# Two-layer graph attention on one core: moving five of sixteen destination blocks of the edge counting to ScalarE's steps, and re-dealing the first stage's order

## The chip, the core and the metric

The kernel runs on one core of a Trainium2 chip. The engines are TensorE (PE, with its weight loads shown as PEld), VectorE (DVE), ScalarE (ACT), GpSimd (POOL) and SyncE (SP); each takes its instructions in the order in which they were recorded and waits on semaphores where an instruction needs another engine's result. The metric is the device time of one execution in microseconds (us); the time given is the median over runs. All times below, unless said otherwise, are from the start of the span of the one profiled execution.

## What is computed

512 nodes with 768 features, 16896 edges sorted by destination (512 of them self loops). Layer 1 has 8 heads of 768 columns, layer 2 has one:

```
def gat_layer(x, W, a_s, a_d, b, edge_index, concat):
    h = (x @ W).reshape(n, H, C)
    alpha_s = einsum('nhc,hc->nh', h, a_s);  alpha_d = einsum('nhc,hc->nh', h, a_d)
    e = leaky_relu(alpha_s[src] + alpha_d[dst], 0.2)
    m = segment_max(e, dst);  e = exp(e - m[dst])
    alpha = e / (segment_sum(e, dst)[dst] + 1e-16)
    out = segment_sum(h[src] * alpha[:, :, None], dst)
    return out + b
h = elu(gat_layer(x, W1, a_src1, a_dst1, b1, ...));  out = gat_layer(h, W2, ...)
result = layernorm(x + out)
```

Since the edges enter only through the attention sums, the kernel turns them once into a dense 512 x 512 matrix of counts (how many edges lead from node s to node d), and from then on works with dense matrices.

## The kernel before

**Heads.** Everything is done head by head in float32. Each large product (x by W1, attention by features, features by W2) is done with seven half-size products P1 to P7 in place of eight, with sums of the operands made by VectorE or by accumulating DMAs. One such half product is three matmuls of 128x384 (`product`, L301-306), run twice (i = 0, 1, the two halves of 128 rows).

**The first stage** (up to about 62.6 us) does three things side by side: it loads and transposes x, it makes head 0's projection and the first four products of head 1's, and it counts the edges. The counting works on 132 chunks of 128 edges. For a chunk there are two one-hot matrices: 32 columns for the destination within a block of 32 nodes (`odw`, made for a quarter of the chunks at once by L493), and 512 columns for the source (`os`). A matmul of the two (L543) adds the chunk to the 32 rows of its block in a PSUM bank. Four blocks of 32 rows make a tile t of 128 destinations; the four column groups of TensorE take a matmul each, so `count` (L532-550) keeps four queues, one for each place of a block in its tile, and takes one from each in a round.

**Two kinds of source matrix.** For tiles 0, 1 and 3 VectorE makes `os` as "node equals source" (L517). For tile S = 2 ScalarE makes it as Sign(node + 0.5 - source) (L515), a step from -1 to 1; the counts of tile 2 then come out as steps, and `counted_by_steps` (L399-406) takes them out of PSUM with half weight (L403, L404, on ScalarE), subtracts neighbours (L405, on VectorE) and makes the mask `absent` (L406). For the other tiles `counted` (L394-397) copies counts and mask straight out of PSUM on ScalarE. A chunk whose edges may fall into two blocks is counted in both; where one of these is a step block and the other isn't, it needs both kinds. All `os` tiles of both kinds come from one pool of 32 buffers (L513); a buffer is free again when the last matmul that reads it is done.

**The order** is written out by hand (L566-617). The chunks are dealt into nine batches (L569: how many of the other tiles', how many of tile 2's). For each batch n the loop records: VectorE's one-hots of the batch, with the sums of products that had been waiting put into their middle (`sources`, L522-528); extra work (operand sums, and `logits`, two passes over 768 columns for each tile of nodes); the batch's projection products (`items`, up to `wants[n]`), each followed by ScalarE's copy out of PSUM and by a share of ScalarE's steps for batch n+1 (`ahead`, L599-601); and then the counting matmuls of batch n. When a tile of destinations is complete, its `counted` instructions are recorded right there (L547-550). After the last batch's products come `spread(0)` (four transposes that lay out the source logits), and then the head loop.

**Names.** In the texts c0 to c8 are the counting matmuls of batches 0 to 8; P1, P5, P3 ... without a mark are head 0's products, P1', P2', P6' head 1's. D0 to D8 are VectorE's one-hots of a batch.

**Around it.** `turn_x` (L200-206) transposes half a tile of x on TensorE into one of three PSUM buffers and copies it out on ScalarE. The P6 and P7 products of head 0 accumulate on the banks `held` that P1 used; VectorE's L428 empties the bank before the next product may start. `nidx` (L505) is the bias of ScalarE's steps. The loads of the stage go through SP's queue (L90, L144, L146, L148, L151, L158) and, for half of x, ScalarE's queue (L143); eight DMA semaphores are used in turn, so a load waits until the eighth before it has landed.

Of the kernel before, what the change touches and what calls it, by code (L numbers as in the profile page):

```python
# [13 lines left out]
AF = mybir.ActivationFunctionType  # L14
ALU = mybir.AluOpType
# [5 lines left out]
NO_EDGE = -1e30  # L21
# [15 lines left out]
def gat_pass(  # L37
# [16 lines left out]
    nc = tc.nc  # L54
# [83 lines left out]
    def block(m, r, cols):  # L138
        return m[r * HK * P:(r + 1) * HK * P, cols].rearrange("(k p) d -> p k d", p=P)

    w1_0 = w1[:, :D]
    for r, cols in enumerate((L, R)):
        nc.scalar.dma_start(x_sb[:, :2, cols], x[:2 * P, cols].rearrange("(t p) d -> p t d", p=P))  # L143
        nc.sync.dma_start(W1[0][r][:, :, L], block(w1_0, r, L))  # L144
    for t in (2, 3):
        nc.sync.dma_start(x_sb[:, t, :], x[t * P:(t + 1) * P, :])  # L146
    b1_rows = ohp.tile([H * DC, P], F32, name="b1_rows")
# [63 lines left out]
    if general:  # L211
        nc.vector.tensor_copy(idx_f, idx_i)
        idx = ohp.tile([P, 2, EC], F32, name="idx")
        psi = tr.tile([P, 512], F32, name="tr")
        for j in range(2):
            for r in range(2):
                nc.tensor.transpose(psi[:, (2 * j + r) * EH:(2 * j + r + 1) * EH], idx_f[:, j, r, :],
                                    ident[:EH, :EH])
        nc.vector.tensor_copy(idx, psi[:, :2 * EC].rearrange("p (j c) -> p j c", j=2))
    else:  # L220

        B, SLACK = 32, 10
        blocks = []
        for c in range(EC):
            m = (c + 0.5) * P * N / E
            b = int(m // B)
            lo, hi = b - (m - b * B < SLACK), b + ((b + 1) * B - m < SLACK)
            blocks.append(range(max(lo, 0), min(hi, N // B - 1) + 1))  # L230
        at = [0]
        for b in blocks:
            at.append(at[-1] + len(b))
        NB = at[EC]
        assert NB + EC <= 512 and max(map(len, blocks)) <= 2


        pick = ohp.tile([EH, NB], F32, name="pick")
        base = ohp.tile([P, NB], F32, name="base")
        lo = 0  # L240
        while lo < EC:
            hi, k = lo + 1, len(blocks[lo])
            while hi % EH and blocks[hi] == blocks[lo]:
                hi += 1
            copy = nc.vector.tensor_copy if lo < 5 * EC // 8 else nc.scalar.copy
            copy(pick[:, at[lo]:at[hi]].rearrange("p (c k) -> p c k", k=k),
                 ident[:EH, lo % EH:(hi - 1) % EH + 1].unsqueeze(2).to_broadcast([EH, hi - lo, k]))
            for j, b in enumerate(blocks[lo]):
                nc.gpsimd.memset(base[:, at[lo]:at[hi]].rearrange("p (c k) -> p c k", k=k)[:, :, j], float(b * B))
            lo = hi  # L250
        nc.vector.tensor_copy(idx_f, idx_i)
        turn_x(0, 0)
        turn_x(1, 0)
        psi = tr.tile([P, 512], F32, name="tr")
        for r in range(2):
            cols = slice(at[r * EH], at[(r + 1) * EH])
            nc.tensor.matmul(psi[:, cols], idx_f[:, 0, r, :], pick[:, cols], start=True, stop=True)
        for r in range(2):
            nc.tensor.transpose(psi[:, NB + r * EH:NB + (r + 1) * EH], idx_f[:, 1, r, :], ident[:EH, :EH])
        rel = ohp.tile([P, NB], F16, name="rel")  # L260
        nc.vector.tensor_tensor(rel, psi[:, :NB], base, op=ALU.subtract)
        idx = ohp.tile([P, EC], F32, name="idx")
        nc.vector.tensor_copy(idx, psi[:, NB:NB + EC])
# [132 lines left out]
        nc.scalar.copy(cnt[:, t, :], ps[:, :N])  # L396
        nc.scalar.activation(absent[:, t, :], ps[:, :N], AF.Relu, bias=far, scale=NO_EDGE)

    def counted_by_steps(t, ps):  # L399


        steps = ohp.tile([P, N + 1], F32, name="steps")
        nc.scalar.activation(steps[:, 1:], ps[:, :N], AF.Copy, scale=0.5)  # L403
        nc.scalar.activation(steps[:, :1], ps[:, N - 1:N], AF.Copy, scale=-0.5)  # L404
        nc.vector.tensor_tensor(cnt[:, t, :], steps[:, 1:], steps[:, :N], op=ALU.subtract)  # L405
        nc.scalar.activation(absent[:, t, :], cnt[:, t, :], AF.Relu, bias=far, scale=NO_EDGE)  # L406

    def first_projection(h, XA, B_):

# [65 lines left out]
    if not general:  # L475


        S = 2
        order = {False: [], True: []}
        for g in range(NT):  # L480
            rs = [[c for c in range(EC) if int((c + 0.5) * P * N / E) // B == b] for b in range(g * 4, g * 4 + 4)]
            while any(rs):
                order[g == S] += [r.pop(0) for r in rs if r]
        hits = {}
        for b in (b for bs in blocks for b in bs):
            hits[b] = hits.get(b, 0) + 1
# [15 lines left out]
            nc.vector.scalar_tensor_tensor(below, rel, 0.0, below, op0=ALU.is_ge, op1=ALU.mult, accum_out=found)  # L502

        nidx = ohp.tile([P, EC], F32, name="nidx")
        nc.scalar.activation(nidx, idx, AF.Copy, bias=0.5, scale=-1.0)  # L505

        def by_steps(b):
            return b * B // P == S

        hot = {}  # L510

# [20 lines left out]
        def count(batch, rest):  # L532


            for c, b in ((c, b) for c in batch for b in blocks[c]):
                queues[b * B % P // B].append((c, b, hot[c, by_steps(b)]))
            while any(queues) and (rest or all(queues) or sum(map(len, queues)) > 3):
                for c, b, h_ in [q_.pop(0) for q_ in queues if q_]:
                    t, r = b * B // P, b * B % P
                    if t not in cps:  # L540
                        pool, name = (bc, "bc") if t == S else (tr, "tr")
                        cps[t] = pool.tile([P, 512], F32, name=name)
                    nc.tensor.matmul(cps[t][r:r + B, :N], od[:, at[c] + b - blocks[c][0], :], h_,  # L543
                                     start=todo[b] == hits[b], stop=todo[b] == 1,
                                     tile_position=(0, r), skip_group_check=True)
                    todo[b] -= 1
            for t in range(NT):  # L547
                if t not in done and all(todo[b] == 0 for b in range(t * P // B, (t + 1) * P // B)):
                    (counted_by_steps if t == S else counted)(t, cps[t])
                    done.add(t)  # L550


# [13 lines left out]
        B1 = {}  # L566
        wants = [3, 4, 7, 10, 12, 14, 16, 18]
        batches = []
        for ours, theirs in ((16, 0), (8, 8), (8, 8), (12, 4), (12, 4), (12, 4), (13, 3), (14, 2), (4, 0)):  # L569
            take = [order[k][:m] for k, m in ((False, ours), (True, theirs))]  # L570
            del order[False][:ours], order[True][:theirs]
            batches.append(take[0][:ours // 2] + take[1] + take[0][ours // 2:])
        assert not any(order.values())
        pos, made, quarter, waiting = 0, set(), EC // NT, []
        for n, batch in enumerate(batches):
            for k in sorted({c // quarter for c in batch} - made):
                destinations(k * quarter, (k + 1) * quarter)
                made.add(k)
            sources(kinds(batch, False), waiting)
            ahead = kinds(batches[n + 1], True) if n + 1 < len(batches) else []  # L580
            items_here = max(wants[n] - pos if n < len(wants) else 0, 1)
            share = -(-len(ahead) // items_here)
            waiting = []
            for f in extra.pop(n, []):
                f()
            while n < len(wants) and pos < wants[n]:
                if pos == wholes:
                    pairs = projection(1, XA, B1)
                    items += [(m, e, False) for m, e in pairs[:4]]
                multiply, empty, on_vector = items[pos]  # L590
                multiply()
                if on_vector:
                    waiting.append(empty)
                else:
                    empty()
                pos += 1
                for t, r in turns.get(pos, []):
                    turn_x(t, r)
                for c in ahead[:share]:  # L599
                    one_hot(c, True)  # L600
                del ahead[:share]
            assert not ahead
            if n == 2:
                turn_b1()
            if n + 1 == len(batches):
                spread(0)
                q = [lift(0, t) for t in range(NT)]
                for t in range(NT - 1):
                    leak(q[t])
                for t in range(NT - 1):  # L610
                    rank(q[t], t)
            if n == 0:
                pst = mm.tile([P, 512], F32, name="mm")
                nc.tensor.matmul(pst[:1, :1], found, ones, start=True, stop=True)
            if n == 3:
                again = nc.values_load(flag[:1, :1], min_val=0, max_val=E)
            count(batch, n + 1 == len(batches))
# [475 lines left out]
```

## Time and profile before

| | us |
|---|---|
| median of 3 runs | 650.8 (650.75 to 650.86) |
| the profiled execution | 650.37 |
| its span, first to last instruction | 648.6 |
| TensorE busy in the span | 637.7 |
| VectorE busy | 519.6 |
| ScalarE busy | 277.3 |
| granted TensorE clock | 0.999 |

A row of the profile names a line of the kernel, an engine, an operation and the tiles it writes and reads; the bracket behind a row says how long the engine had been idle before it and what ended that. The stretches view gives each engine's busy time in a stretch of the span. The waits view adds up who waited for whom.

### The profile page before, as it was taken

How to read it: one execution, taken by the hardware profiler on the slowest of the kernel's cores; microseconds unless marked ns; L12 is line 12 of the kernel's file. 1: busy time of each engine (PE TensorE's matmuls, PEld its weight loads, DVE VectorE, ACT ScalarE, POOL GpSimd, SP SyncE). 2: the span in 40 equal slices, each digit the busy share in tenths (PEclk: the TensorE clock that was granted, in tenths of full speed). 3: DMA queues.
4: the chain of work that ended last, by engine and by line, in shares of the span. 5: the costliest groups of instructions: out<-in, count | busy, mean ns of one | idle time of the engine just before them, and what ended most of it. 6: DMA issues, size and time to landing. Idle time of an engine off the chain costs nothing.

```text
span 648.6 us, 7216 instructions
## 1 busy us (share of the span) xinstructions
PE 637.7 (98%) x2383; PEld 405.0 (62%) x2383; DVE 519.6 (80%) x1141; ACT 277.3 (43%) x482; POOL 48.3 (7%) x90
## 2 busy tenths in 40 slices
PE   8999999999999999999999999999999999999995
PEld 4544586556765586556765586556755586644553
DVE  7989989977779677877779687877779687876775
ACT  6774744530726045430726045430726045243440
POOL 1310020011000110011000110011000110000000
PEclk9999999999999999999999999999999999999999
DMA  9993499197806792196806792196706892000122
GB/s 318 328 203 86 75 327 292 35 256 207 202 0 153 170 277 97 33 260 200 205 1 149 174 277 98 33 258 204 202 1 153 218 254 97 25 1 1 29 61 76
DMA packets 77640, 97.95 MB, mean 151 GB/s; under 512 B 37094, under 2 KB 60446, under 8 KB 77598
## 3 DMA queue, kind: packets, MB, share of 16 engines
q1 hardware_dynamic: 63934, 75.80, 37.5%
q0 software_dynamic: 12976, 20.65, 18.4%
q10 hardware_dynamic: 688, 0.98, 0.4%
q8 instruction: 21, 0.34, 0.2%
q14 instruction: 21, 0.17, 0.1%
HBM read 85.09 MB, written 1.57 MB: 134 GB/s over the span
## 4 chain that ended last, share of the span: by engine, by line
PE 96%; ACT 1%; DMA 1%; DVE 1%; issue 0%; SPq 0%
PE mm L305 64%; PE mm L764 20%; PE mm L710 3%; PE mm L1039 3%; PE held L305 2%; PE tr L543 1%; DMA w<-in_L_gnn_W_dram 1%; ACT os L515 1%; PE bc L446 0%; PE bc L543 0%; PE tr L963 0%; PE tr L679 0%; ACT xT L205 0%; DVE os L517 0%; PE bc L985 0%
## 5 line engine op out<-in xcount | busy, mean ns | idle before, releaser
L305 PE MATMUL mm<-w,gT 128*128 128x384 f32 x288 | 97.5, 488 | 0.0
L305 PE MATMUL mm<-w,xT 128*128 128x384 f32 x264 | 88.2, 488 | 0.0
L305 PEld LDWEIGHTS mm<-w,gT 128*128 128x128 f32 x288 | 54.0, 190 | 35.2 <-issue 1.6
L305 PEld LDWEIGHTS mm<-w,xT 128*128 128x128 f32 x264 | 50.0, 190 | 35.4 <-ACT os L515 0.8
L768 ACT COPY u<-mm 128x256 f32<-128x256 f32 x21 | 7.8, 372 | 142.0 <-PE mm L764 142.0
L463 ACT ACTIVATE q<-q,nmax 128x512 f32<-128x512 f32 x36 | 25.8, 721 | 89.8 <-DVE nmax L461 89.8
L764 PE MATMUL mm<-PT,hs 128*128 128x256 f32 x252 | 61.4, 380 | 0.0
L305 PE MATMUL mm<-w1t,gS 128*128 128x384 f32 x180 | 60.7, 486 | 0.0
L305 PE MATMUL mm<-w2t,xS 128*128 128x384 f32 x168 | 56.6, 487 | 0.0
L764 PEld LDWEIGHTS mm<-PT,hs 128*128 128x128 f32 x252 | 47.9, 190 | 8.3 <-issue 0.4
L363 DVE TENSOR_TENSOR h<-h,mm 128x384 f32<-128x384 f32 x72 | 39.7, 551 | 14.6 <-PE mm L305 14.0
L305 PEld LDWEIGHTS mm<-w1t,gS 128*128 128x128 f32 x180 | 34.2, 190 | 23.5
L305 PEld LDWEIGHTS mm<-w2t,xS 128*128 128x128 f32 x168 | 31.9, 190 | 22.4 <-ACT q L452 0.4
L764 PE MATMUL mm<-pS,gS 128*128 128x256 f32 x168 | 43.3, 380 | 0.0
L687 ACT COPY nr<-q 128x1024 uint16<-128x1024 uint16 x32 | 33.4, 1044 | 22.9 <-DVE q L673 15.8
L692 ACT COPY PT<-zr 128x1024 uint16<-128x1024 uint16 x32 | 37.1, 1160 | 2.0 <-DMA zr<-nr 2.0
L764 PEld LDWEIGHTS mm<-pS,gS 128*128 128x128 f32 x168 | 31.9, 190 | 4.7 <-DVE pS L737 0.4
L305 PE MATMUL mm<-w,gS 128*128 128x384 f32 x96 | 32.6, 486 | 0.0
L305 PE MATMUL mm<-w1t,gT 128*128 128x384 f32 x96 | 32.5, 488 | 0.0
L305 PE MATMUL mm<-w,xS 128*128 128x384 f32 x96 | 32.5, 488 | 0.0
L106 POOL DMA_DIRECT2D w1t<-in_L_gnn_W_dram x7 | 8.9, 1267 | 311.3 <-DVE hs L727 97.8
L363 DVE TENSOR_TENSOR u<-u,mm 128x384 f32<-128x384 f32 x28 | 15.4, 553 | 19.0 <-PE mm L305 18.7
(189 smaller groups left out, 1086.1 us busy)
## 6 DMA issues: line engine op xcount, KB each, us to landing
w<-in_L_gnn_W_dram SPq DMA_DIRECT2D x90, 384.0 KB, 6.1
w<-in_L_gnn_W_dram POOLq DMA_DIRECT2D x16, 576.0 KB, 9.5
w2t<-in_L_gnn_W_dram SPq DMA_DIRECT2D x10, 576.0 KB, 4.9
w1t<-in_L_gnn_W_dram SPq DMA_DIRECT2D x9, 576.0 KB, 4.6
w2t<-in_L_gnn_W_dram POOLq DMA_DIRECT2D x8, 576.0 KB, 9.8
w1t<-in_L_gnn_W_dram POOLq DMA_DIRECT2D x7, 576.0 KB, 8.7
a_s<-in_L_gnn_a_src_dram SPq DMA_DIRECT2D x8, 384.0 KB, 3.7
a_d<-in_L_gnn_a_dst_dram SPq DMA_DIRECT2D x8, 384.0 KB, 4.1
```

Of the source, the lines that this page charges most:

```text
L106: nc.gpsimd.dma_start(t1, upper[:, :, R], accum_op=ALU.add)
L305: nc.tensor.matmul(ps[:, :HALF], A_[p][:, k, i * P:(i + 1) * P], B_[p][:, k, :], start=start and k == 0, stop=k == HK - 1, skip_group_chec ...
L363: nc.vector.tensor_tensor(a, a, ps, op=ALU.subtract if p == "P7" else ALU.add)
L463: nc.scalar.activation(q, q, AF.Exp, bias=nmax, scale=-1.0)
L515: nc.scalar.activation(o, nodes, AF.Sign, bias=nidx[:, c:c + 1])
L543: nc.tensor.matmul(cps[t][r:r + B, :N], od[:, at[c] + b - blocks[c][0], :], h_, start=todo[b] == hits[b], stop=todo[b] == 1, tile_position ...
L687: nc.scalar.copy(apart.rearrange("p (h n) -> p h n", h=2), q.bitcast(U16).rearrange("p (n h) -> p h n", h=2))
L692: nc.scalar.copy(PT.rearrange("p s n -> p (s n)").bitcast(U16).rearrange("p (s n h) -> p s n h", s=NT, h=2)[:, :, t * P:(t + 1) * P, :], p ...
L710: nc.tensor.matmul(ps[:, :N], HS[h][:, s, c * P:(c + 1) * P], PT[:, s, :], start=(s == 0), stop=(s == NT - 1))
L764: nc.tensor.matmul(bank[p][:, :HN], A_[p][:, k, c * P:(c + 1) * P], B_[p][:, k, :], start=over is None and k == 0, stop=k == 1, skip_group ...
L768: nc.scalar.copy(u, part("P1"))
L1039: nc.tensor.matmul(ps[:, :cols.stop - cols.start], PT[:, s, t * P:(t + 1) * P], h2[:, s, cols], start=(s == 2), stop=(s == 1))
```

## The change

- **First W1 part in three loads** (L144): the left half of the upper W1 block is loaded as three DMAs of 128 x 384, one for each k, in place of one of 128 x 3 x 384. Two DMAs more go through SP's queue and the eight semaphores.
- **Indices ahead of x's second transpose** (L253): `turn_x(1, 0)` is recorded after the four matmuls that turn the edge indices.
- **A fifth step block**: block 4 (the first 32 destinations of tile 1) joins the blocks 8 to 11 of tile 2. Tile 1 is then taken out of PSUM twice: by `counted` for all 128 rows, and then by `counted_by_steps` for the first 32 rows, which overwrites them. `counted_by_steps` takes the rows it is for.
- **Batches dealt anew**: block 4's chunks go into batches 3 to 5, tile 2's last chunks into batch 6 in place of 7, so that tile 2 is complete after c6. Some batches have 17 chunks, batch 7 has 13.
- **ScalarE's order**: `nidx` is recorded after the first product's copy and two copies of x; in batch 0 fewer steps stand ahead of the copies of x (2 of 9 after each of three products, the last 3 behind the loop).

VectorE's one-hots per batch are 16, 10, 9, 12, 13, 13, 13, 15, 4 before (105) and 16, 10, 9, 13, 10, 14, 13, 13, 4 after (102); ScalarE's steps per batch are 0, 8, 8, 4, 4, 8, 5, 2, 0 before (39) and 0, 9, 10, 10, 7, 10, 7, 0, 0 after (53). The rounds of four counting matmuls are 6, 6, 7, 7, 5, 9, 7, 6, 4 before and 6, 6, 7, 8, 5, 9, 7, 5, 4 after, 57 in both.

```diff
-        nc.sync.dma_start(W1[0][r][:, :, L], block(w1_0, r, L))
+        for ks in (slice(0, 1), slice(1, 2), slice(2, HK)) if r == 0 else (slice(0, HK),):
+            nc.sync.dma_start(W1[0][r][:, ks, L], block(w1_0, r, L)[:, ks])
...
         turn_x(0, 0)
-        turn_x(1, 0)
         psi = tr.tile([P, 512], F32, name="tr")
...
             nc.tensor.transpose(psi[:, NB + r * EH:NB + (r + 1) * EH], idx_f[:, 1, r, :], ident[:EH, :EH])
+        turn_x(1, 0)
...
-    def counted_by_steps(t, ps):
+    def counted_by_steps(t, ps, rows):
         steps = ohp.tile([P, N + 1], F32, name="steps")
-        nc.scalar.activation(steps[:, 1:], ps[:, :N], AF.Copy, scale=0.5)
-        nc.scalar.activation(steps[:, :1], ps[:, N - 1:N], AF.Copy, scale=-0.5)
-        nc.vector.tensor_tensor(cnt[:, t, :], steps[:, 1:], steps[:, :N], op=ALU.subtract)
-        nc.scalar.activation(absent[:, t, :], cnt[:, t, :], AF.Relu, bias=far, scale=NO_EDGE)
+        nc.scalar.activation(steps[rows, 1:], ps[rows, :N], AF.Copy, scale=0.5)
+        nc.scalar.activation(steps[rows, :1], ps[rows, N - 1:N], AF.Copy, scale=-0.5)
+        nc.vector.tensor_tensor(cnt[rows, t, :], steps[rows, 1:], steps[rows, :N], op=ALU.subtract)
+        nc.scalar.activation(absent[rows, t, :], cnt[rows, t, :], AF.Relu, bias=far[rows], scale=NO_EDGE)
...
-        S = 2
+        S, S1 = 2, 1
+        stepped = {*range(S * P // B, (S + 1) * P // B), S1 * P // B}
...
-        nc.scalar.activation(nidx, idx, AF.Copy, bias=0.5, scale=-1.0)
         def by_steps(b):
-            return b * B // P == S
+            return b in stepped
...
-                    (counted_by_steps if t == S else counted)(t, cps[t])
+                    if t != S:
+                        counted(t, cps[t])
+                    if t in (S, S1):
+                        counted_by_steps(t, cps[t], slice(0, P if t == S else B))
...
-        for ours, theirs in ((16, 0), (8, 8), (8, 8), (12, 4), (12, 4), (12, 4), (13, 3), (14, 2), (4, 0)):
-            take = [order[k][:m] for k, m in ((False, ours), (True, theirs))]
-            batches.append(take[0][:ours // 2] + take[1] + take[0][ours // 2:])
+        for ours, theirs, first in ((16, 0, 0), (8, 8, 0), (8, 8, 0), (10, 4, 3), (10, 3, 3), (11, 4, 2), (11, 6, 0),
+                                    (13, 0, 0), (4, 0, 0)):
+            batches.append(order[:ours // 2] + steps_s1[:first] + steps_s[:theirs] + order[ours // 2:ours])
...
-            share = -(-len(ahead) // items_here)
+            share = len(ahead) // (items_here + 1) if n == 0 else -(-len(ahead) // items_here)
...
+                if pos == 1:
+                    nc.scalar.activation(nidx, idx, AF.Copy, bias=0.5, scale=-1.0)
                 for c in ahead[:share]:
                     one_hot(c, True)
                 del ahead[:share]
-            assert not ahead
+            for c in ahead:
+                one_hot(c, True)
```

More of the change, by code (lines that the diff above doesn't have):

```diff
@@ L475, in gat_pass, with in_turn @@
     if not general:
-        S = 2
-        order = {False: [], True: []}
+        S, S1 = 2, 1
+        stepped = {*range(S * P // B, (S + 1) * P // B), S1 * P // B}
+        order, by_block = [], {}
+        for c in range(EC):
+            by_block.setdefault(int((c + 0.5) * P * N / E) // B, []).append(c)
+        def in_turn(blocks_):
+            lists = [list(by_block[b]) for b in blocks_]
+            while any(lists):
+                yield from [r.pop(0) for r in lists if r]
         for g in range(NT):
-            rs = [[c for c in range(EC) if int((c + 0.5) * P * N / E) // B == b] for b in range(g * 4, g * 4 + 4)]
-            while any(rs):
-                order[g == S] += [r.pop(0) for r in rs if r]
+            order += in_turn(b for b in range(g * P // B, (g + 1) * P // B) if b not in stepped)
+        steps_s, steps_s1 = list(in_turn(range(S * P // B, (S + 1) * P // B))), list(in_turn([S1 * P // B]))
         hits = {}
@@ L568, in gat_pass @@
         batches = []
-        for ours, theirs in ((16, 0), (8, 8), (8, 8), (12, 4), (12, 4), (12, 4), (13, 3), (14, 2), (4, 0)):
-            take = [order[k][:m] for k, m in ((False, ours), (True, theirs))]
-            del order[False][:ours], order[True][:theirs]
-            batches.append(take[0][:ours // 2] + take[1] + take[0][ours // 2:])
-        assert not any(order.values())
+        for ours, theirs, first in ((16, 0, 0), (8, 8, 0), (8, 8, 0), (10, 4, 3), (10, 3, 3), (11, 4, 2), (11, 6, 0),
+                                    (13, 0, 0), (4, 0, 0)):
+            batches.append(order[:ours // 2] + steps_s1[:first] + steps_s[:theirs] + order[ours // 2:ours])
+            del order[:ours], steps_s[:theirs], steps_s1[:first]
+        assert not order and not steps_s and not steps_s1
         pos, made, quarter, waiting = 0, set(), EC // NT, []
```

## The prediction

> **What bounds the kernel now.** I read the page's busy times first, then the chain of work that ended last in order of time, then the stretches, and then the timelines of VectorE and ScalarE in the first stage, because the change touches nothing behind it.
>
> ```profile
> PE 637.7 (98%) x2383; PEld 405.0 (62%) x2383; DVE 519.6 (80%) x1141; ACT 277.3 (43%) x482; POOL 48.3 (7%) x90
> ```
>
> TensorE works 98% of the span, so time can be gained or lost only where it waits. Behind 62.68 us the chain is TensorE without a gap worth naming up to 82; in the first stage the largest wait stands at its end:
>
> ```profile
> 59.52 0.03 PE bc L543
> 59.56 0.02 issue
> 59.58 0.60 ACT steps L403
> 60.18 0.07 ACT steps L404
> 60.25 0.02 issue
> 60.27 0.69 DVE cnt L405
> 60.96 1.06 DVE os L517 x4
> 62.03 0.04 issue
> 62.07 0.61 PE tr L543 x3
> ```
>
> Tile 2 is complete after c7, ScalarE takes it out, VectorE subtracts (L405), and only then makes the last four one-hots, for which c8 waits. VectorE's queue is in order: whoever stands behind L405 waits for ScalarE. The stretches (columns: stretch, PE, PEld, DVE, ACT, POOL busy, clock, DMA) tell how much room VectorE has:
>
> ```profile
> 45.00:50.00 5.00, 5.00 (x42) 2.47 (x41) 4.96 (x17) 4.82 (x9) 1.26 (x1) 1.00 0.48 92
> 50.00:55.00 5.00, 5.00 (x38) 2.44 (x37) 4.83 (x13) 2.20 (x4) 0.26 (x1) 1.00 0.61 118
> 55.00:60.00 5.00, 5.00 (x37) 2.41 (x36) 4.88 (x16) 1.38 (x3) 0.00 (x0) 1.00 0.02 5
> ```
>
> None: from 45 to 60 us it is as full as TensorE. A microsecond that it idles here ends up behind D8, and so in the time. VectorE's and ScalarE's timelines give the prices:
>
> ```profile
> 41.47 0.62 DVE L517 TENSOR_SCALAR os<-nodes,idx 128x512 bf16<-128x512 f16 x2 [0.73 <-PE tr L543]
> 42.00 1.01 DVE L428 TENSOR_TENSOR hs<-hs,held 128x384 f32<-128x384 f32 x2
> 46.64 3.50 DVE L517 TENSOR_SCALAR os<-nodes,idx 128x512 bf16<-128x512 f16 x13
> ...
> 16.77 6.23 ACT L515 ACTIVATE os<-nodes,nidx 128x512 bf16<-128x512 f16 x10
> 23.77 0.48 ACT L426 COPY hs<-mm 128x384 f32<-128x384 f32 x1 [0.76 <-PE mm L305]
> 48.66 0.57 ACT L396 COPY cnt<-tr 128x512 f32<-128x512 f32 x1
> 49.12 0.69 ACT L397 ACTIVATE absent<-tr,far 128x512 bf16<-128x512 f32 x1
> ```
>
> From start to start, a one-hot takes 0.267 us on VectorE, a step 0.617 on ScalarE, a copy of 128x384 0.37, L396 0.47, L397 0.58, L403 with L404 0.69 (59.58 to 60.27), L405 0.61 (60.27 to 60.88), a pair of logits 2.0. The first of these rows also shows a buffer wait: c4's matmuls start at 41.04, and the one-hot that needs the first one's buffer starts 0.43 later.
>
> **The change, step by step.** The order in which the changed program's instructions stand on each engine, with the instruction that each waits for, is known; I put the durations above on it.
>
> *Start.* TensorE waits 0.77 us for the W1 block (L144, issued 1.69, landed 7.38). The next block of its size lands 1.57 later, so thirds are about 0.5 apart: 6.3, 6.9 and 7.4. The products need them at 6.75, 7.4 and 8.1, so P1 starts at 6.75 instead of 7.52. Ends: nothing, if the first third is not early, and 0.77; I take 0.77. Two more DMAs push later ones back on the eight semaphores: x's tiles 2 and 3 are issued when x's first load has landed (0.82 + 3.4 = 4.2) and not at 2.67. The engines still work on the W1 blocks until 8.95, which covers it; without cover x would land 1.5 later than its 9.9, before its use at 13.3. The Trainium skill, "DMA: Bandwidth & Descriptors", section "Rules for kernel authors", speaks against the split: many small transfers should be coalesced into one. Its fixed cost of about 2.0 us for each DMA would, as an estimate, make two more transfers cost up to 4 us, if nothing hid them.
>
> *Indices.* Three transposes (0.12 apart) leave the way of VectorE's `rel`: 6.64 becomes 6.27, and VectorE, busy without a gap to 30 us, is 0.37 earlier.
>
> *ScalarE before c0.* With two steps fewer ahead, x's third and fourth copies no longer wait for it: they start 0.59 after their transposes (as 15.43 to 16.02 before), at 13.87 instead of 14.90, and end at 15.73. c0 starts at 15.5 instead of 16.56. P5 then waits for VectorE's L285 (20.92 less 0.37): 20.6 instead of 21.6. Up to here 1.0 us is won.
>
> *ScalarE behind it.* Now 15 steps instead of 10 stand between x's copies and the copy of P5's first bank: 15.73 + 15 x 0.617 = 24.99, where before it idled 0.76 and started at 23.77. P3 goes on top of that bank and starts 0.53 after the copy does: 25.5, before 25.50. The gain is spent.
>
> *Buffers.* ScalarE's steps are made a batch ahead and hold more of the 32 buffers. D4's first five one-hots now wait for the second to ninth matmul of c3 (before, D4's first six found c2's buffers free at 31.5). Behind them in VectorE's queue stand both L428 that P7 needs. c3 at 35.37: 0.43 + 5 x 0.267 = 1.76, L428 at 37.13, P7 0.60 later (42.00 to 42.60 before): 37.74, before 37.04. At c4 (41.81) the same with the last three of seven: 42.24 + 0.80 + 0.60 = 43.64 for P4, before 42.60. So c5 starts at 47.71, 1.04 later than before. No waiting at all would make this nothing.
>
> *The fifth block's subtraction.* It is the term that decides. L405 for tile 1's 32 rows stands in VectorE's queue ahead of all of D6, and waits for ScalarE to take tile 1 out of PSUM after c5. VectorE is there at 43.04 + 0.94 (two L428) + 7 x 0.267 + 2.0 = 47.85. ScalarE copies P4's first bank at 45.85 (2.21 after P4's start, as 7.52 to 9.73), then 4 steps, a copy, 3 steps: 50.91; then 0.47 + 0.58 + 0.69: L405 starts at 52.65. **VectorE idles 4.8 us.** No row has an instruction on 32 partitions. Ends: nothing, and the price of 128; I take the 128 rows, since the cast of 66x512 (L251, 0.42) is near the 128x512 of L673 (0.49). With nothing, 1.3 us less.
>
> *The rest.* VectorE from 52.65: 0.61, D6 3.47, logits 3.95, tile 2's L405 0.61 (ScalarE long done), D7 3.47, logits 2.0: D8 starts at 66.76 instead of 60.88. P6' follows D8's start by 1.73, as before: 68.45 against 62.61, **5.8 us later**. The relief of VectorE is small: 3 one-hots, 0.80 us, less 0.61 for the new L405, because chunks that reach into a neighbouring block need both kinds. Finishing tile 2 a batch sooner does take the wait at 59.56 away, about 1.1 us with the four one-hots; what is late next is VectorE itself. The Trainium skill, "Perfetto Trace Analysis", section "Optimizing Scalar/DVE Operations", says that with a saturated VectorE, giving work to ScalarE may make sense. By that rule alone the 3 one-hots would give 650.0; the order says that the work moved brings a wait six times its size.
>
> Behind P6', TensorE is without a gap and everything moves with it; ScalarE's and VectorE's chain of the first softmax starts 0.3 us earlier against P6' than before (behind D8's four one-hots without waiting for ScalarE, 0.31 in the row of 62.33), so nothing is added there. The profiled execution's own 650.37 (span 648.6 and 1.8 around it) becomes 656.2; the median of the runs stands 0.43 above it: **656.6**.
>
> **The rivals.**
>
> 1. *The hold is shorter.* ScalarE is in time, buffers bind less. L405 can't start before c5's 28th of 33 matmuls is out (1.7 + 0.4 behind c5's start) and ScalarE's 1.74 have passed: 3.8 after c5, against 4.94 in the forecast. With that, P6' is 1.1 earlier (4.7 lost: 655.5); with c5 where it was before as well, 3.7 lost: 654.5; with the 32-row prices at nothing besides, 653.2. For it: VectorE's slack is read off one profile. Against: ScalarE's row 45 to 50 is full (4.82 of 5) before it gets more.
> 2. *Faster.* VectorE's idling costs nothing, because TensorE is the bound and VectorE runs ahead of it: in 40 to 45 it was busy 4.27 of 5. Then TensorE's own waits go, 0.77, 0.56, 0.30 and the 1.1 at the end: 2.7 us, 648.1. This decides if VectorE had as much room between 45 us and D8 as the change makes it idle more. Against: the three stretches above leave it 0.33 us of 15, and the forecast needs 4.8.
> 3. *Nothing.* The gains at both ends and a hold of half my size meet: within 1.3 us of 650.8.
> 4. *More.* The first softmax, or buffers in c6 and c7, add waits that I didn't see: 658.5.
>
> **Chances.** Forecast (655.9 to 657.4) 0.56; rival 1 (653.2 to 655.9) 0.27; rival 4 0.09; rival 2 0.04; rival 3 0.04. A measurement here tells 0.2%, 1.3 us, from no change. Faster 0.04, same 0.04, slower 0.92. Range: 653.7 to 658.2, which leaves out rivals 2 and 3, the end of rival 1 where 32 rows are free, and most of 4.
>
> **What would show it.** In the changed profile: L305 at 6.75 without a DMA wait; P5 at about 20.6; ScalarE's copy of P5's bank at 25 without idling; VectorE's waits for L543 of 3 us ahead of 36; and above all the 32x512 L405, some 4.8 us of idle time ahead of it, ended by ScalarE's step, and c6 and c7 waiting for one-hots. P6' at 68. Wrong it is, if VectorE's wait ahead of that subtraction is under 2 us, or if TensorE passes c7 without waiting for VectorE.

## The result and the profile after

The changed kernel takes **656.13 us** (median of 6 runs, 655.87 to 656.62); the kernel before took 650.83 beside it (650.73 to 651.04). The ratio is 1.0083, 95% interval 1.0072 to 1.0093. The profiled execution took 656.31 us with a span of 654.5, at a granted clock of 0.997. From the start of P6' to the end of the span it is 585.83 us, before 585.99: the whole loss lies ahead of P6', in the first stage. Of the five step blocks, the four of tile 2 were ScalarE's before; the change moves one, block 4.

The busy times of the page, for the changed kernel:

```profile
PE 641.4 (98%) x2383; PEld 405.0 (62%) x2383; DVE 519.7 (79%) x1139; ACT 286.4 (44%) x499; POOL 46.0 (7%) x90
```

VectorE has two instructions fewer and the same work, ScalarE 9 us more. What ended last is told by the chain in order of time (start, us, what):

```profile
46.40 0.48 ACT hs L428
46.88 2.46 ACT os L524 x4
49.34 0.36 ACT hs L428
49.70 1.85 ACT os L524 x3
51.55 0.47 ACT cnt L398
52.01 0.59 ACT absent L399
52.60 0.46 ACT steps L405
53.06 0.06 ACT steps L406
53.12 0.02 issue
53.15 0.68 DVE cnt L407
53.82 3.42 DVE os L526 x13
57.24 0.89 DVE scr L322 x2
...
61.12 0.60 DVE cnt L407
61.73 3.42 DVE os L526 x13
...
67.02 1.06 DVE os L526 x4
68.08 0.04 issue
68.13 0.61 PE tr L552 x3
```

Before, from 45 us on, the chain needed VectorE only for tile 2's subtraction and the last four one-hots. Now it leaves TensorE at 46.4, goes on ScalarE through P4's two copies (L428), seven steps and tile 1's way out of PSUM, and stays on VectorE from 53.15 to 68.08. The stretches show the same hole (columns as in the prediction's: PE, PEld, DVE, ACT, POOL):

```profile
45.00:50.00 5.00, 5.00 (x44) 2.50 (x42) 3.26 (x10) 3.60 (x7) 0.56 (x1) 1.00 0.52 100
50.00:55.00 5.00, 5.00 (x26) 2.51 (x22) 1.85 (x6) 4.25 (x10) 0.30 (x1) 1.00 0.61 118
55.00:60.00 5.00, 4.61 (x30) 2.25 (x28) 4.93 (x14) 0.96 (x3) 0.00 (x0) 1.00 0.00 0
60.00:65.00 5.00, 3.98 (x21) 1.34 (x20) 4.96 (x18) 1.47 (x3) 0.00 (x0) 1.00 0.02 5
65.00:70.00 5.00, 3.78 (x21) 1.81 (x19) 4.96 (x13) 2.42 (x4) 0.00 (x0) 1.00 0.48 146
```

VectorE was busy 4.96 and 4.83 of 5 us in the first two; now it is 3.26 and 1.85. TensorE starves only later, from 55 on, when what VectorE didn't make is needed. Its timeline and ScalarE's name the places:

```profile
36.35 1.40 DVE L526 TENSOR_SCALAR os<-nodes,idx 128x512 bf16<-128x512 f16 x5 [2.65 <-PE tr L552]
37.67 1.01 DVE L430 TENSOR_TENSOR hs<-hs,held 128x384 f32<-128x384 f32 x2
53.15 0.68 DVE L407 TENSOR_TENSOR cnt<-steps 32x512 f32<-32x512 f32 x1 [4.85 <-ACT steps L406]
```

```profile
16.23 9.30 ACT L524 ACTIVATE os<-nodes,nidx 128x512 bf16<-128x512 f16 x15
25.43 0.46 ACT L428 COPY hs<-mm 128x384 f32<-128x384 f32 x1
52.49 0.57 ACT L405 ACTIVATE steps<-tr 32x512 f32<-32x512 f32 x1
```

And TensorE's rows with a wait behind 25 us:

```profile
25.94 2.20 PE L307 MATMUL mm<-w,xS 128*128 128x384 f32 x6 [0.81 <-ACT hs L428]
38.27 4.14 PE L307 MATMUL held<-w,xT 128*128 128x384 f32 x12 [0.47 <-DVE hs L430]
44.16 4.14 PE L307 MATMUL held<-w1t,xT 128*128 128x384 f32 x12 [0.56 <-DVE hs L430]
56.77 0.64 PE L552 MATMUL tr<-os,odw 128*32 128x512 bf16 x2 [0.39 <-DVE os L526]
62.31 0.66 PE L552 MATMUL tr<-os,odw 128*32 128x512 bf16 x4 [0.50 <-DVE os L526]
63.36 2.23 PE L552 MATMUL tr<-os,odw 128*32 128x512 bf16 x14 [0.39 <-DVE os L526]
67.34 1.40 PE L552 MATMUL tr<-os,odw 128*32 128x512 bf16 x8 [0.94 <-DVE os L526]
```

### The profile page after: what moved, and what is told of

Its sections match the earlier page's. It is cut to its first block, busy times and chain, and to the rows that moved or that the text cites. A ratio compares the mean times of both kernels' runs of the same rounds, so it can differ in the third digit from the quotient of the medians.

```text
span 654.5 us, 7232 instructions
## 1 busy us (share of the span) xinstructions
PE 641.4 (98%) x2383; PEld 405.0 (62%) x2383; DVE 519.7 (79%) x1139; ACT 286.4 (44%) x499; POOL 46.0 (7%) x90
## 4 chain that ended last, share of the span: by engine, by line
PE 92%; DVE 3%; ACT 3%; DMA 1%; issue 0%; SPq 0%; DVEq 0%; ACTq 0%
PE mm L307 62%; PE mm L779 20%; PE mm L725 3%; PE mm L1054 3%; PE held L307 2%; ACT os L524 2%; DVE os L526 1%; DMA w<-in_L_gnn_W_dram 1%; DVE scr L322 1%; PE tr L552 0%; PE bc L448 0%; PE tr L978 0%; PE tr L694 0%; PE mm L206 0%; DVE cnt L407 0%
## 5 line engine op out<-in xcount | busy, mean ns | idle before, releaser
L524 ACT ACTIVATE os<-nodes,nidx 128x512 bf16<-128x512 f16 x53 | 33.6, 720 | 0.0
L526 DVE TENSOR_SCALAR os<-nodes,idx 128x512 bf16<-128x512 f16 x102 | 28.6, 350 | 3.7 <-PE tr L552 3.7
```

The costliest lines, as they stand in the source:

```text
L524: nc.scalar.activation(o, nodes, AF.Sign, bias=nidx[:, c:c + 1])
L526: nc.vector.tensor_scalar(o, nodes, idx[:, c:c + 1], None, op0=ALU.is_equal)
```

## The experiments

Theory: VectorE's idling ahead of the 32-row subtraction is the main loss, and it comes from that instruction's place in the queue; buffers cost about 1 us, and ScalarE's 15 steps ahead of P3 use up what was won at the start. Rival S: ScalarE's 14 more steps are the loss, and the idling only shows them. Rival B: the 32 buffers are the loss.

Each profile is read as three stretches of TensorE's timeline: from P1 to c0, from c0 to c5 and from c5 to P6'. A start that scatters between executions blurs them less than the times themselves; P1 to c0 still holds waits for W1 (9.38 in e3), and c0 to c5 a wait of P5 for VectorE where c0 is early (0.33 in e7). The rest, P6' to the end of the span, is 585.8 to 586.3 in all twelve. "Against before" is the difference of medians to the runs of the kernel before on the same chip (650.65 for e1 to e4, 650.86 for e5 to e8, 650.83 for the others).

| kernel | P1 | P1 to c0 | c0 to c5 | c5 to P6' | median | against before | ratio, 95% interval |
|---|---|---|---|---|---|---|---|
| before | 7.52 | 9.04 | 30.11 | 15.94 | 650.83 | | |
| changed | 6.96 | 9.06 | 32.21 | 20.44 | 656.13 | +5.30 | 1.0083 [1.0072, 1.0093] |
| e1_late32 | 6.57 | 8.75 | 32.23 | 16.89 | 652.59 | +1.94 | 1.0030 [1.0020, 1.0039] |
| e2_bufs44 | 6.48 | 8.65 | 31.04 | 20.43 | 655.19 | +4.54 | 1.0069 [1.0052, 1.0086] |
| e3_late_both_44 | 6.61 | 9.38 | 31.05 | 14.57 | 649.15 | -1.50 | 0.9976 [0.9966, 0.9986] |
| e4_early_only | 7.57 | 8.65 | 30.30 | 15.94 | 649.99 | -0.66 | 0.9989 [0.9980, 0.9999] |
| e5_sooner | 7.86 | 9.05 | 30.10 | 16.27 | 651.28 | +0.42 | 1.0006 [0.9997, 1.0016] |
| e6_sooner_late | 7.86 | 9.05 | 30.10 | 14.68 | 649.79 | -1.07 | 0.9985 [0.9976, 0.9994] |
| e7_composite | 7.06 | 8.65 | 30.51 | 14.68 | 648.97 | -1.89 | 0.9972 [0.9961, 0.9984] |
| e8_composite_44 | 7.24 | 8.65 | 30.14 | 14.56 | 648.07 | -2.79 | 0.9960 [0.9946, 0.9974] |
| e9_three_loads | 6.72 | 9.18 | 30.17 | 15.94 | 650.26 | -0.57 | 0.9994 [0.9984, 1.0003] |
| e10_order_only | 7.51 | 8.72 | 30.11 | 15.93 | 650.49 | -0.34 | 0.9996 [0.9987, 1.0005] |

**e1: only the place of the subtraction.** In the changed kernel, `counted_by_steps` returns its last two instructions instead of recording them. Tile 2's are still recorded at once; the loop records tile 1's later, the subtraction behind D6 and its logits, the mask behind batch 7's items:

```diff
-                        counted_by_steps(t, cps[t], slice(0, P if t == S else B))
+                        put_off[t] = counted_by_steps(t, cps[t], slice(0, P if t == S else B))
...
+            if n == 6:
+                put_off[S1][0]()
...
+            if n == 7:
+                put_off[S1][1]()
```

> The changed kernel with only the place of the fifth block's subtraction altered: tile 1's 32-row L407 stands in VectorE's queue behind D6 and the two pairs of logits that follow it, and its mask (L408) in ScalarE's queue behind the items of batch 7. ScalarE has just as many steps as in the changed kernel. Theory (VectorE is held at its place in the queue): the 4.85 us of idling ahead of L407 go, P6' comes at 64.5 instead of 68.67 us, and the time is near 652.0, 4.1 less than the changed kernel's 656.1; what is left above the kernel before is the idling for buffers and the fifth block's own cost. Rival (ScalarE's 14 more steps are the cost, and the hold only shows them) or rival (the 32 buffers are starved): at most 1 us is won, 655 or more.

652.59 (652.0 expected), 3.5 less than the changed kernel, with every step still on ScalarE. Rival S, which allowed 1 us, falls as the main cause. VectorE's timeline:

```profile
47.97 3.51 DVE L527 TENSOR_SCALAR os<-nodes,idx 128x512 bf16<-128x512 f16 x13 [0.37 <-PE tr L554]
...
55.35 0.68 DVE L407 TENSOR_TENSOR cnt<-steps 32x512 f32<-32x512 f32 x1
56.81 0.69 DVE L407 TENSOR_TENSOR cnt<-steps 128x512 f32<-128x512 f32 x1 [0.79 <-ACT steps L406]
```

The 32-row subtraction no longer waits, D6 runs at 47.97 instead of 53.75, and TensorE passes c6 and c7 without a wait. Of the 4.85 us, 0.37 and 0.79 came back as other waits (4.85 - 0.37 - 0.79 = 3.69; the stretch c5 to P6' shrank by 3.55). The 0.79 is a new one: ScalarE's own row says that it could not take tile 2 out, since tile 1's subtraction still held what it writes:

```profile
56.12 0.60 ACT L405 ACTIVATE steps<-bc 128x512 f32<-128x512 f32 x1 [1.87 <-DVE cnt L407]
```

**e2: only the buffers.** In the changed kernel, both allocations of one-hots:

```diff
-            hot[c, steps] = o = ohp.tile([P, N], BF16, name="os", bufs=32)
+            hot[c, steps] = o = ohp.tile([P, N], BF16, name="os", bufs=44)
...
-                o2 = ohp.tile([P, N], BF16, name="os", bufs=32)
+                o2 = ohp.tile([P, N], BF16, name="os", bufs=44)
```

> The changed kernel with 44 instead of 32 buffers for one-hots, and nothing else. Theory (the hold at the 32-row subtraction is the main loss, buffers a small one): VectorE's 1.08 and 2.65 us of waiting for c2's and c3's matmuls go, P7 and P4 come about 1.0 us earlier, c5 at about 47.1 instead of 48.23, and the hold stays at 4.9 us, since tile 1 is complete only behind c5: about 655.0, 1.1 less than the changed kernel. Rival (buffers are the main loss): 652 or less. Rival (buffers cost nothing, since VectorE has to wait for tile 1 anyway): 656.1.

655.19; rival B falls too. c0 to c5 is 1.17 shorter, as expected, and c5 to P6' is the same (20.43 against 20.44). I had expected the idle time at the subtraction to stay at 4.9. It grew:

```profile
51.08 0.68 DVE L407 TENSOR_TENSOR cnt<-steps 32x512 f32<-32x512 f32 x1 [5.78 <-ACT steps L406]
```

VectorE came there at 45.30, 0.9 earlier against c5 than in the changed kernel, and the subtraction started 4.91 behind c5 (46.17), there 4.92 (48.23). So the place fixes the *end* of the idling, and a faster VectorE only waits longer. What the buffers brought came through P7 and P4, not through VectorE's time.

**e3: both subtractions late, and 44 buffers.** e1 and e2 together, with tile 2's subtraction behind D8 as well and its mask behind the last lifts (`lift` is ScalarE's first pass of the first softmax):

```diff
+            if n == 8:
+                put_off[S][0]()
...
+                put_off[S][1]()
```

> The changed kernel with both subtractions off VectorE's path (tile 1's behind D6 and its logits, tile 2's behind D8, their masks on ScalarE behind the items of batch 7 and behind the last lifts) and 44 buffers. All 14 more steps of ScalarE stay. Theory: the hold, the buffer waits and the 0.6 us of tile 2's subtraction ahead of D8 are gone together: P6' at about 61.7, 649.9 us. Rival (ScalarE's steps are the cost): 652 or more, with ScalarE's copies of the products' banks late.

649.15 (649.9 expected): faster than before, with all 14 more steps on ScalarE. The changed kernel's loss was in its waits. From 45 to 70 us TensorE has no gap in e3's stretches:

```profile
45.00:50.00 5.00, 5.00 (x43) 2.45 (x42) 4.96 (x18) 4.79 (x9) 1.24 (x1) 1.00 0.49 95
50.00:55.00 5.00, 5.00 (x40) 2.42 (x39) 4.83 (x13) 2.85 (x8) 0.00 (x0) 1.00 0.62 120
55.00:60.00 5.00, 5.00 (x31) 2.42 (x30) 4.97 (x18) 2.09 (x5) 0.00 (x0) 1.00 0.05 17
60.00:65.00 5.00, 5.00 (x26) 2.79 (x24) 4.75 (x12) 4.09 (x8) 0.00 (x0) 1.00 0.40 143
65.00:70.00 5.00, 5.00 (x17) 2.98 (x16) 4.71 (x16) 3.12 (x6) 0.00 (x0) 1.00 0.16 29
```

The last expectation of rival S, that ScalarE's copies come late, did show in one place, the copy of P5's first bank, for which P3 waits (TensorE's row):

```profile
25.93 2.20 PE L307 MATMUL mm<-w,xS 128*128 128x384 f32 x6 [0.83 <-ACT hs L429]
```

**e4: only the early part**, on the kernel before:

```diff
-        nc.sync.dma_start(W1[0][r][:, :, L], block(w1_0, r, L))
+        for ks in (slice(0, 1), slice(1, 2), slice(2, HK)) if r == 0 else (slice(0, HK),):
+            nc.sync.dma_start(W1[0][r][:, ks, L], block(w1_0, r, L)[:, ks])
...
-        turn_x(1, 0)
...
+        turn_x(1, 0)
...
-        nc.scalar.activation(nidx, idx, AF.Copy, bias=0.5, scale=-1.0)
...
-            share = -(-len(ahead) // items_here)
+            share = len(ahead) // (items_here + 1) if n == 0 else -(-len(ahead) // items_here)
...
+                if pos == 1:
+                    nc.scalar.activation(nidx, idx, AF.Copy, bias=0.5, scale=-1.0)
...
-            assert not ahead
+            for c in ahead:
+                one_hot(c, True)
```

> The kernel before with only the early part of the change: W1's first block in three loads, the transposes of x's second block behind the indices', ScalarE's negated indices moved, and fewer steps ahead of c0. No fifth block, and the deal of before. Theory: P1 starts 0.56 us earlier as in the changed kernel, P5 0.5 to 0.6 earlier, ScalarE idles ahead of its copy of P5's bank as before, and the gain reaches c8 but for what VectorE, which is as full as before from 45 us on, can't follow: about 650.2, 0.6 less than the kernel before. Rival (the early part itself costs, by the two more loads or by steps that ScalarE makes later): 651.3 or more.

649.99, 0.66 less than before, as expected. Two things on the way were not as expected: P1 started at 7.57 in this profile, not 0.56 earlier, and ScalarE did not idle ahead of its copy of P5's bank. It has 12 steps here between x's copies and that copy, and just keeps up: P3 starts without a wait, where 15 steps made it wait 0.8.

```profile
16.43 7.46 ACT L515 ACTIVATE os<-nodes,nidx 128x512 bf16<-128x512 f16 x12
23.79 0.46 ACT L427 COPY hs<-mm 128x384 f32<-128x384 f32 x1
```

**e5: only tile 2 a batch sooner**, on the kernel before:

```diff
-        for ours, theirs in ((16, 0), (8, 8), (8, 8), (12, 4), (12, 4), (12, 4), (13, 3), (14, 2), (4, 0)):
+        for ours, theirs in ((16, 0), (8, 8), (8, 8), (12, 4), (12, 4), (12, 4), (13, 5), (14, 0), (4, 0)):
```

> The kernel before with the deal of the last batches alone altered: batch 7 takes (13, 5) and batch 8 (14, 0) instead of (13, 3) and (14, 2), so that tile 2 is complete after c6 and its subtraction L405 stands ahead of D7, as in the changed kernel. No fifth block, no early part. Theory (a subtraction is paid for where VectorE's queue reaches it): the wait of c8 at the end of the stage goes, but VectorE reaches L405 about 1.1 us before ScalarE has taken tile 2 out, and this lands behind D8: 651.5, 0.7 to 0.9 more than the kernel before. Rival (sooner is a gain, since tile 2's subtraction no longer stands between c7 and the last four one-hots): 649.7.

651.28, and the interval of its ratio takes in 1: no difference that the timing can tell, and no gain. VectorE's wait ahead of L405 moved, as expected, from 59.9 to here (0.90, not 1.1):

```profile
55.60 0.69 DVE L405 TENSOR_TENSOR cnt<-steps 128x512 f32<-128x512 f32 x1 [0.90 <-ACT steps L404]
```

The wait of c8 was expected to go and did not: VectorE, held up earlier, came late with D8 instead. TensorE's rows, the kernel before and e5:

```profile
61.28 1.39 PE L543 MATMUL tr<-os,odw 128*32 128x512 bf16 x8 [0.74 <-DVE os L517]
...
62.17 1.18 PE L543 MATMUL tr<-os,odw 128*32 128x512 bf16 x7 [0.94 <-DVE os L517]
```

**e6: e5 with the subtraction behind D8.** The same deal, and tile 2's two last instructions put off as in e3:

```diff
-                    (counted_by_steps if t == S else counted)(t, cps[t])
+                    if t == S:
+                        put_off.extend(counted_by_steps(t, cps[t]))
+                    else:
+                        counted(t, cps[t])
...
+            if n == 8:
+                put_off[0]()
...
+                put_off[1]()
```

> As the run with the deal alone, and with tile 2's subtraction put behind D8 in VectorE's queue and its mask behind the last lifts in ScalarE's. Theory: neither the hold nor the 0.6 us of the subtraction stand ahead of D8 any more; 0.36 of idling and 0.61 of work go from the path: 649.8, 0.9 less than the kernel before. Rival (the first softmax needs the counts of tile 2 at once, so that the subtraction is late there): 650.7, no gain.

649.79. c5 to P6' falls from 16.27 to 14.68 by the place of one 0.61 us instruction (its mask on ScalarE moved with it), and c8 no longer waits. The first softmax doesn't miss it: the rest is 586.1 as elsewhere.

**e7 and e8: both gains without the fifth block**, e4's edit and e6's together on the kernel before, with 32 buffers (e7), and with e2's edit too (e8).

> The early part of the change and tile 2 a batch sooner with its subtraction behind D8, on the kernel before: the changed kernel without its fifth block, 32 buffers. Theory: the two gains, 0.66 measured for the early part and 0.9 expected for the late one, add up, since one moves c0 to c5 and the other the end of the stage: 649.1. Rival (they take the same idle time of TensorE away): 649.8.

> As the composite, with 44 buffers for one-hots: against the changed kernel with both subtractions late and 44 buffers (649.15) it lacks only the fifth block's steps and their deal. Theory (the fifth block relieves VectorE by 3 one-hots less a subtraction, 0.2 us, and costs ScalarE 8.6 us on the way to P3): VectorE's 0.73 us of waiting for a buffer in batch 4 and TensorE's 0.30 behind it go, and the time is the same as with the fifth block or up to 0.5 less: 648.6 to 649.2. Rival (the fifth block is a gain once nothing waits for its subtraction): 649.6 or more.

648.97, and **648.07** for e8, 0.5 below the range expected; it is the best here, 8.1 us less than the changed kernel. The gains add up in e7 (0.66 + 1.07 = 1.73; 1.89 measured). e8 differs from e3 only in the fifth block's steps and their deal. It is 0.91 shorter from c0 to c5 and equal behind (14.56 and 14.57); by the medians 1.3 less, and the intervals of the two ratios overlap. Of the 0.91, 0.59 lie between c0 and P3, which doesn't wait here, and 0.22 between c3 and c4, where c3 has one round of matmuls less. TensorE's row of P3 in e8:

```profile
25.24 2.10 PE L306 MATMUL mm<-w,xS 128*128 128x384 f32 x6
```

So, as dealt here, the fifth block brings nothing, even where nobody waits for its subtraction, and costs about 0.9.

**e9 and e10: the early part in halves.** e9 is e4's first three lines alone on the kernel before, e10 is all of e4's edit but these:

```diff
-        nc.sync.dma_start(W1[0][r][:, :, L], block(w1_0, r, L))
+        for ks in (slice(0, 1), slice(1, 2), slice(2, HK)) if r == 0 else (slice(0, HK),):
+            nc.sync.dma_start(W1[0][r][:, ks, L], block(w1_0, r, L)[:, ks])
```

> The kernel before with W1's first block in three loads, and nothing else of the early part. Theory (the products start when their third has landed, and what is behind is held by the engines' order): TensorE's wait for W1 (0.77 us in the profile of before) goes, but c0 still waits for x's copies behind ScalarE's steps, so that little of it arrives: 650.5 to 650.9, none to 0.3 less. Rival (two loads more cost on the queue): 651.3 or more. Rival (the start alone carries the whole early gain of 0.66): 650.2.

> The early part without the three loads: the transposes of x's second block behind the indices', the negated indices moved, and fewer steps ahead of c0, with W1's first block in one load. Theory: x's third and fourth copies no longer wait for ScalarE, c0 comes up to 0.5 us earlier, and it is this that carries most of the early part's 0.66: 650.3. Rival (it is the loads that do it): 650.8.

650.26 and 650.49. Both intervals take in 1, so the timing doesn't tell which half carries the 0.66; no loss by the loads is seen. e9's median lies below the range expected and near the rival's 650.2; e10's lies between its forecast and its rival. The profiles show what each does. With the loads alone P1 starts at 6.72 without a wait, but x's second pair of transposes still waits 0.56 for ScalarE; with the order alone that wait is 0.24, and P1 starts at 7.51. P1 to c0 is 9.18 and 8.72, 9.04 before. In e9 the wait for ScalarE did not swallow the gain, though the theory said that it would: ScalarE's work ahead of c0 starts with its copy of P1's first half (9.07, before 9.73), so all of it moved along, and c0 came at 15.90, 0.66 earlier than before. TensorE's rows, e9 first:

```profile
6.72 2.31 PE L306 MATMUL held<-w,xT 128*128 128x384 f32 x6
...
14.78 0.93 PE L205 MATMUL mm<-ident,hs 128*128 128x128 f32 x6 [0.56 <-ACT xT L206]
```

```profile
7.51 2.17 PE L305 MATMUL held<-w,xT 128*128 128x384 f32 x6 [0.30 <-ACT xT L205]
...
15.10 0.93 PE L204 MATMUL mm<-ident,hs 128*128 128x128 f32 x6 [0.24 <-ACT xT L205]
```

## Why the prediction was right

The time (656.13 for 656.6) and the mechanism held. Step by step, the profile of the changed kernel against the numbers of the prediction:

- *Start.* P1 without a DMA wait at 6.96 instead of 6.75. The gain is 0.56, not 0.77, and a part of it is lost inside P1: its first half (i = 0; its three matmuls are six records in the profile) takes 2.50, before 2.17. x's tiles 2 and 3 were issued at 4.80 (forecast 4.2, before 2.67), and TensorE did not wait for them. In e3 the wait stands in the middle of P1 (0.47, for W1); in e4 P1 starts at 7.57 in spite of the three loads, since TensorE's transposes ahead of it end late.
- *Indices.* **Missed.** The 0.37 did not come: `rel` started at 6.69, not 6.27. The transposes did leave its way (from VectorE's cast of the indices to `rel` it is 1.40 us, before 2.00), but the indices landed later and took it back: the cast stood at 5.29, before at 4.64. That is scatter and not the change: with the old order the cast stands at 5.27 and 5.29 in e5 and e6 too, and where it came early with the new one, at 4.89 and 4.81 in e1 and e2, `rel` is at 6.29 and 6.21. But the order alone doesn't settle it: with a late cast the old order can lose nothing (in e9 it is 1.39 from cast to `rel`), and in e4, with the new order and the cast at 4.93, the first three transposes took 0.85 (0.49 in e1) and `rel` came at 7.09. P5 stood at 20.99, forecast 20.6.
- *c0* came 0.54 earlier in the profiled execution (16.02), not 1.06 (15.5). One execution is a poor ruler for this term: over the seven profiles with the whole early part c0 stands at 15.13 to 16.22, 15.75 in the mean, over the three with the old start (before, e5, e6) at 16.56 to 16.91, 16.79. That is 1.04, but how much of it is chance these few profiles don't tell.
- *ScalarE behind it.* 15 steps, then the copy of P5's bank at 25.43 without idling, P3 at 25.94 (forecast 24.99 and 25.5; 0.44 late, as c0 was by 0.52). "The gain is spent" holds: from c0 to P3 it is 9.94 in e3 and 9.35 in e8, 0.59 for the three steps more.
- *Buffers.* c5 was to be 1.04 later for them; c0 to c5 fell by 1.17 with 44 buffers. The 2.65 ahead of 36.35 is the wait that the sum has; the 1.08 ahead of 28.69, which it lacks, only took from that wait and held up no product.
- *The subtraction.* VectorE arrived at 48.3 (forecast 47.85) and started it at 53.15 (52.65): 4.85 of idling for 4.8. The open price of 32 partitions, between nothing and that of 128, was that of 128: 0.68 against 0.69 us for the subtraction, 0.57 against 0.60 for L405.
- *The rest.* D8 at 66.94 (66.76), P6' at 68.67 (68.45): 6.06 later for 5.8. Two misses cancel in part here: from c0 to the subtraction everything stood about 0.5 later than forecast, and from the subtraction to D8 it took 13.79 and not 14.11. The 0.43 added between the profiled execution and the median did not repeat either: the changed kernel's profiled execution took 656.31 (forecast 656.2), 0.18 more than its median. That the median came within 0.5 is in part luck; the hold itself, 4.85 for 4.8, is not.
- *Tile 2 sooner.* "What is late next is VectorE itself": e5 shows it, no gain until the subtraction leaves VectorE's way (e6).

Of the rivals, the first (a shorter hold) named 3.8 us behind c5 as the least; it was 4.92. The 1.1 between them is ScalarE's own queue, which came to tile 1 only at 51.45, behind the seven steps. The second (VectorE's idling costs nothing) falls with e1, where 3.5 us came back as soon as the idling was gone. But the gains that it listed are there to be had: e8, without the fifth block, is 2.8 us faster than the kernel before, and the list adds up to 2.7. The parts fit less well than the sum: the end of the stage (c5 to P6') gave 1.38 for the 1.1 listed, and of the 0.56 ahead of x's last transposes 0.24 stayed. The third rival falls with the time itself, 5.3 above, and the fourth with the rest behind P6', 585.83 against 585.99, and with D8 to P6', which took the 1.73 of the forecast.

The rule of the Trainium skill that the prediction weighed, "Perfetto Trace Analysis", section "Optimizing Scalar/DVE Operations" (with a saturated VectorE, some work may go to ScalarE), did not carry here: e3 against e8 has the 3 one-hots moved with no wait for a subtraction, and is not faster but 0.9 slower in the stretch c0 to c5. And of "DMA: Bandwidth & Descriptors", section "Rules for kernel authors", which would rather coalesce transfers: e9 shows no cost of two more loads beyond its interval (ratio 0.9984 to 1.0003). Of the up to 4 us that the prediction estimated from the page's 2.0 us for each DMA, nothing shows in it.

What stays open: how the 0.66 of the early part divides between loads and order, whether the fifth block would pay with fewer steps ahead of P3, and how much of the hold would go if ScalarE took tile 1 out ahead of its seven steps; no run tried another deal or another order of ScalarE for it.

## What to carry to other kernels

On an engine that works in order, price an instruction by where it stands: the time at which its last input can be there less the time at which the engine gets there; here an instruction of 0.6 us kept VectorE idle for 4.85 ahead of D6 and for nothing behind it (though in e1, at its later place, it held up ScalarE, and VectorE then waited 0.79 for that). Moving work to an idle engine is worth nothing if what comes back has to pass through the busy one's queue, or if the extra work stands ahead of a copy that TensorE waits for. Before giving such an idea up, move the dependent instruction behind the next independent work and see what is left.

## What the runs showed of the hardware

- In three operations here, 32 partitions took what 128 take: 0.68 and 0.69 us for VectorE's f32 subtraction over 512 columns, 0.57 and 0.60 for ScalarE's copy out of PSUM, 0.72 and 0.72 for the mask (L408). Fewer partitions bought next to no time.
- The first microseconds scatter between executions. The cast of the indices stands between 4.64 and 5.56. The six 128x128 transposes ahead of the indices' take 0.89 us in the kernel before and 1.48 in e5, the same instructions at a granted clock of 1.00 in both; no run here says why. By the seven profiles with the same early part, whose c0 stands at 15.13 to 16.22, a start read off one profile is good to some 0.5 us either way.
